# Attention of a two-layer graph network: two visits a round with eight heads each in place of four with four

## The chip, the cores and the metric

The kernel runs on one core of one Trainium2 chip. The metric is device time in microseconds (us) of one execution. Engines are named as the profile names them: PE is TensorE, with PEld its weight loads; DVE is VectorE, ACT is ScalarE, POOL is GpSimd, SP is SyncE, which here issues the transfers. SBUF and PSUM are the two on-chip memories; PSUM is used as eight banks of 128 x 512 numbers.

## The reference

64 graphs of 256 nodes with 512 features share one adjacency matrix. Cut to what matters:

```python
# x (64, 256, 512), adj (256, 256), all float32; 8 heads of 64
h = relu(layernorm(x))
q, k, v = h @ Wq + bq, h @ Wk + bk, h @ Wv + bv
scores = einsum('bqhd,bkhd->bhqk', q, k) / 8 + (1 - adj) * -1e9
x = x + einsum('bhqk,bkhd->bqhd', softmax(scores), v) @ Wo + bo
h = relu(layernorm(x))
hW = h @ W
e = leaky_relu(hW @ a1 [:, :, None] + hW @ a2 [:, None, :], 0.2) * adj
x = x + elu(softmax(e) @ hW + beta * hW)
```

## The kernel before

The graphs are worked off in 32 pairs. Every large product (Q and K, V, the output projection O, and W of the second layer) is done for a pair of graphs in Strassen's way (the Winograd form): seven block products, called `p(1)` to `p(7)` of a `Unit`, in place of eight. For a pair `p` the units are `UnitQK(p, 0)` and `UnitQK(p, 1)` (`ua`, `ub`), `UnitV(p)` (`uv`), `UnitO(p)` (`uo`) and `UnitW(p)` (`uw`). The block sums of the left operand are made by `combine_31`, `combine_2` and `combine_4` (L304, L308 and others).

A product is eight matmul records of PE of 256 columns (a float32 matmul of the code shows as two records). It goes to one PSUM bank. Products 2 and 3 have none of their own: they add into the banks of products 1 and 5. So product 3 can start only when the results that need product 5 alone have been read from that bank; for Q and K `put2` does this (L374, on DVE), and `put2` in turn needs the sum `u3` (L288).

Attention is done per graph `b` and half `q` of the heads (four heads). `scores(b, q)` makes four score tiles on PE (L420, two heads side by side in tiles of 64 x 128), then exp on ACT (L424), the product with the mask on POOL (L425) and the sum of the two halves on POOL (`pp`, L427). `values(b, q)` weighs V with them (`av`, L438, four heads side by side in tiles of 128 x 32), adds up the softmax sums (`sm`, L447), and leaves on DVE the reciprocal (L449), a running sum (L450) and the normalized output (`oT`, L452); a second running sum (L453) is put on POOL by the caller, through `between`, behind the second head of the scores that follow.

A *visit* is one `values` followed by the `scores` of the next graph or half. In the steady state a *round* handles one pair in `first_half(p)` and `second_half(p)`, with four visits in it. The order of PE, DVE, ACT and POOL is the order in which the code is written (`manual_schedule`): each engine takes its instructions in that order and waits where an input or a buffer isn't ready. In a round the stages of three pairs are mixed: Q, K and V of pair p+1, attention of pair p, O and the normalization of pair p-1, and the second layer's W of pair p-2.

Between the second visit of `second_half` and the next rounds, the second layer of pair p-1 is prepared: `y_stats` (L248) and `y_scales` (L255 on DVE, L258 to L260 on POOL) give mean and deviation, `y_normal` (L507, ACT) the normalized rows `h2`, `y_sums` (L513, DVE, tile `pr`) two weighted sums of each row, `gat_scores`, `gat_exp` and `divide` the attention weights of the second layer, `gat_t` their transposes (L546), `gat_z` the product with `h2` (`pz`, L559). Transfers stand on SP's queue in program order: `x` (in `load`), the same rows once more as `y` for the residual (`residual`, which also adds a bias on POOL, L470), and the results.

Tiles of one tag share a fixed number of buffers (`BUFS`, L58). A tile takes over a buffer of an older one and waits until that is no longer read. PSUM has eight banks under one tag.

Of the kernel before, what the change touches and what calls it, by code (L numbers as in the profile page):

```python
# [11 lines left out]
ALU = mybir.AluOpType  # L12
# [11 lines left out]
def kernel(ctx: ExitStack, tc: tile.TileContext, x, adj, wq, bq, wk, bk, wv, bv, wo, bo, w, a, beta, out):  # L24
# [33 lines left out]
    BUFS = {"set": 13, "qk": 8, "v": 4, "pt": 4, "xt": 4, "y": 8, "h2": 4, "e": 2, "eT": 2, "m": 2, "c": 3, "u": 4}  # L58

    def blk(tag, name):  # L60

        return sb([P, 2, N], tag, name, BUFS[tag])

# [12 lines left out]
    def load(p, *which):  # L76
        for g in [2 * p + gi for gi in which or (0, 1)]:
            for t in range(NT):
                XT[g, t] = sb([P, D], "xt", f"x_{g}_{t}", BUFS["xt"])
                nc.sync.dma_start(XT[g, t], x[g, t * P:(t + 1) * P, :])  # L80
# [213 lines left out]
    def combine_31(s, a21, a22, tag="set"):  # L294

        s["tag"] = tag
        s[7] = blk(tag, f"s3_{s['name']}")
        a21(s[7], ALU.subtract, s[1])
        s[5] = blk(tag, f"s1_{s['name']}")
        a22(s[5], ALU.add, s["a21"])  # L300
# [112 lines left out]
    def scores(b, q, between=None):  # L413
        pss = [bank(f"sc_{b}_{q}_{i}") for i in range(4)]
        for pair in range(2):
            qk = QK.pop((b, 2 * q + pair))
            for k in range(NT):
                for h in range(2):
                    hs = slice(h * HD, (h + 1) * HD)
                    nc.tensor.matmul(pss[2 * pair + h][:, k * N:(k + 1) * N], qk[hs, 1, k * P:(k + 1) * P],  # L420
                                     qk[hs, 0, :], start=True, stop=True)
        for i in range(4):
            pt = PT[b, q, i] = blk("pt", f"pt_{b}_{q}_{i}")
            nc.scalar.activation(pt, two(pss[i]), AF.Exp, scale=QSCALE)  # L424
            nc.gpsimd.tensor_tensor(pt, pt, maskT, ALU.mult)  # L425
            pp = PP[b, q, i] = sb([P, N], "pp", f"pp_{b}_{q}_{i}", 4)
            nc.gpsimd.tensor_tensor(pp, pt[:, 0, :], pt[:, 1, :], ALU.add)  # L427
            if between and i in between:
                between[i]()
# [12 lines left out]
    def values(b, q):  # L442

        ps = weigh(V.pop((b, q)), [PT.pop((b, q, i)) for i in range(4)], f"{b}_{q}")
        sums = bank(f"sm_{b}_{q}")
        for i in range(4):
            nc.tensor.matmul(sums[i * HH:(i + 1) * HH, :N], ones[:, :HH], PP.pop((b, q, i)), start=True, stop=True)  # L447
        rec = sb([P, N], "rec", f"rec_{b}_{q}")
        nc.vector.reciprocal(rec, sums[:, :N])  # L449
        nc.vector.tensor_tensor(acc, sums[:, :N], acc, ALU.add)  # L450
        OT[b, q] = blk("set", f"oT_{b}_{q}")
        nc.vector.tensor_tensor(OT[b, q], two(ps), rec.unsqueeze(1).to_broadcast([P, 2, N]), ALU.mult)  # L452
        return lambda: nc.gpsimd.tensor_tensor(acc, acc, rec, ALU.add)  # L453
# [48 lines left out]
    def normal(g, rstd, nmr, tag="h2"):  # L502
        h2 = H2[g] = [sb([P, D], tag, f"h2_{g}_{t}", BUFS[tag]) for t in range(NT)]
        SC[g] = sb([P, NT, 2], "s12", f"s12_{g}", 3)
        for t in range(NT):
            for f in range(2):
                nc.scalar.activation(h2[t][:, f * N:(f + 1) * N], Y[g, f][:, t, :], AF.Relu, bias=nmr[:, t:t + 1],  # L507
                                     scale=rstd[:, t:t + 1])
# [68 lines left out]
    class UnitW(Unit):  # L577

        def __init__(self, p, tags=("m", "c")):
            self.pair, self.o, self.tags = p, {}, tags  # L580
            super().__init__(f"w_{p}", nodes_mm(A.pop(("z", p)), WW))

        def elu(self, gi, fh, src, o=None, step=None):
            g = 2 * self.pair + gi
            if not step:
                m = blk(self.tags[0] if (gi, fh) != (0, 0) else "m", f"m_{g}_{fh}")
                nc.scalar.activation(m, src, AF.Relu, scale=-1.0)
                nc.scalar.activation(m, m, AF.Exp, scale=-1.0)  # L588
                self.o[gi, fh] = (o or blk(self.tags[1], f"o_{g}_{fh}"), m)
            if step is not False:  # L590
                nc.vector.scalar_tensor_tensor(self.o[gi, fh][0], src, 0.0, Y.pop((g, fh)), op0=ALU.max, op1=ALU.add)

        def finish(self, gi, fh, eng):
            g = 2 * self.pair + gi
            o, m = self.o[gi, fh]
# [10 lines left out]
        def put2_sums(self):  # L606
            self.c = blk(self.tags[1], f"o_{2 * self.pair + 1}_1")
# [77 lines left out]
    def residuals(p, tag="y"):  # L685
        for gi, fh in ((0, 0), (1, 1), (1, 0), (0, 1)):
            residual(p, gi, fh, tag)
# [26 lines left out]
    def start():  # L714
# [42 lines left out]
        scores(0, 0)  # L757
# [4 lines left out]
        shift(2)  # L762
        products(uv, 3)
        return wo_blocks

    def first():
        add = values(0, 0)
        scores(0, 1, {1: add})
        x_t(1)
        load(2)  # L770
        s = A["h", 1]
        ua, ub, uv = UnitQK(1, 0), UnitQK(1, 1), UnitV(1)
        ua.p(1)
        combine_24(s)
        products(ua, 4, 6)
        prods = project_a()
        prods(0)
        products(ua, 2, 7)
        add = values(0, 1)
        scores(1, 0, {1: add})  # L780
        residuals(0)
        products(ua, 5)
        ub.p(1)
        prods(1)
        products(ub, 4)
        products(ua, 3)
        products(ub, 6)
        prods(2)
        products(ub, 2)
        add = values(1, 0)  # L790
        scores(1, 1, {1: add})
        products(ub, 7, 5)
        uv.p(1)
        products(ub, 3)
        prods(3)
        prods(4)
        products(uv, 4)
        for i in range(2 * NT):
            x_stats(2, i)
        add = values(1, 1)  # L800
        x_scales(2)
        scores(2, 0, {1: add})
        o_blocks(0)
        products(uv, 6, 2)
        x_normals(2, *range(2 * NT))
        products(uv, 7, 5)
        prods(5)
        products(uv, 3)
        combine_24(A["o", 0])
        uo = UnitO(0)  # L810
        uo.p(1)
        uo.p(4)
        add = values(2, 0)
        scores(2, 1, {1: add})
        products(uo, 6, 2)
        return uo


    def first_half(p):
        g0, g1 = 2 * p, 2 * p + 1  # L820
        uw = UnitW(p - 2)
        uw.p(1)
        x_stats(p + 1, 0)
        x_stats(p + 1, 1)
        uw.p(4)
        x_stats(p + 1, 2)
        x_stats(p + 1, 3)
        products(uw, 6, 2, 7, 5)
# [3 lines left out]
        add = values(g0, 0)  # L832
        scores(g0, 1, {1: add})
# [3 lines left out]
        uo = UnitO(p - 1)  # L837
        uo.p(1)
# [8 lines left out]
        products(uo, 2)  # L847
        return uo

    def second_half(p, uo):  # L850
        g0, g1 = 2 * p, 2 * p + 1
        products(uo, 7)
# [3 lines left out]
        if p + 2 < NP:  # L856
            load(p + 2)
        products(uo, 3)
        combine_2(A["h", p + 1])
        add = values(g0, 1)  # L860
        y_stats_1(p - 1)
        y_stats_2(p - 1)
        combine_4(A["h", p + 1])
        scores(g1, 0, {1: lambda: (add(), y_scales(p - 1))})
        ua, ub = UnitQK(p + 1, 0), UnitQK(p + 1, 1)
        products(ua, 1, 4)
        y_normal(p - 1, 1)
        products(ua, 6)
        y_sums(p - 1, 1, 0, 1)
        products(ua, 2)  # L870
# [3 lines left out]
        add = values(g1, 0)  # L874
        scores(g1, 1, {1: add})
        products(ua, 3)
        y_sums(p - 1, 0, 1)
        products(ub, 1, 4, 6)
        gat_scores(g1 - 2)
        products(ub, 2)  # L880
        gat_exp(g1 - 2)
        gat_scores(g0 - 2)
        gat_exp(g0 - 2)
        products(ub, 7)
        divide(p - 1)
        products(ub, 5)
        add = values(g1, 1)
        scores(g1 + 1, 0, {1: add})
        if p == NP - 2:
            o_blocks(p, "xt")  # L890
        residuals(p)
        uv = UnitV(p + 1)
        uv.p(1)
        gat_t(g1 - 2)
        gat_t(g0 - 2)
        products(ub, 3)
        products(uv, 4, 6, 2, 7, 5)
        if p == NP - 2:
            return uv
        gat_z(p - 1)  # L900
        products(uv, 3)
        combine_24(A["z", p - 1])

    def last(uv):
        p = NP - 1
        g0, g1 = 2 * p, 2 * p + 1
        combine_24(A["o", p - 1])
        add = values(g0, 0)
        scores(g0, 1, {1: add})
        products(uv, 3)  # L910
# [3 lines left out]
        add = values(g0, 1)  # L914
        scores(g1, 0, {1: add})
        products(uo, 5)
        y_stats_1(p - 1)
        gat_z(p - 2)
# [3 lines left out]
        combine_24(A["z", p - 2])  # L922
        add = values(g1, 0)
        scores(g1, 1, {0: lambda: y_normal(p - 1, 1), 1: add})
        uw = UnitW(p - 2, ("pt", "xt"))
        products(uw, 1, 4)
        y_sums(p - 1, 1, 0, 1)
        products(uw, 6)
# [3 lines left out]
        residual(p, 0, 0, "qk")  # L932
        gat_scores(g1 - 2)
        gat_exp(g1 - 2)
        uw.p(5)
        uw.put2_sums()
        add = values(g1, 1)
        o_blocks(p)
        residual(p, 1, 1, "qk")
        residual(p, 1, 0, "qk")  # L940
        residual(p, 0, 1, "qk")
        add()
# [10 lines left out]
    def end(uw, uo):  # L953
        p = NP - 1
        g0, g1 = 2 * p, 2 * p + 1
        products(uo, 2)
        gat_scores(g0 - 2)
        gat_exp(g0 - 2)
        uo.p(6)
# [13 lines left out]
        normal(g1, rstd, minus(mr, f"y{g1}"), "qk")  # L973
# [6 lines left out]
        normal(g0, rstd, minus(mr, f"y{g0}"), "qk")  # L980
# [6 lines left out]
        uw = UnitW(p - 1, ("pt", "xt"))  # L987
# [16 lines left out]
        uw.put2_elu()  # L1004
        uw.p(3)
        gat_t(g0)
        uw.put12()
# [9 lines left out]
        uw = UnitW(p, ("pt", "xt"))  # L1017
# [16 lines left out]
    with tc.manual_schedule(engines={ENG.PE, ENG.DVE, ENG.Activation, ENG.Pool}):  # L1034
        WO = start()
        WW = {}
        uo = first()
        second_half(1, uo)
        for p in range(2, NP - 1):
            uv = second_half(p, first_half(p))  # L1040
        end(*last(uv))
# [16 lines left out]
    def general(src, dst, W, mask):  # L1058
        xt = sb([P, NT, D], "x", "fx", 1)
# [145 lines left out]
```

## Time and profile before

| what | value |
|---|---|
| median of three runs | 2856.71 us (2855.55 to 2857.03) |
| the profiled execution | 2857.51 us, its span 2855.7 us |
| mean granted TensorE clock | 0.997 |
| one round (from the av at 1009.24 to the one at 1097.33) | 88.09 us |
| busy in that round: PE, DVE, ACT, POOL | 88.09, 63.74, 32.63, 50.41 us |
| starts of the visits in and around it (av) | 1009.24, 1024.02, 1040.97, 1077.35, 1097.33 us |
| number of L449 (one for each `values`) | 128 |

How to read it: the span is the time from the first to the last instruction of the profiled execution, and the runs that are timed have no profile. A busy share says how much of the span an engine was at work, not whether others waited for it. A line of the timeline has the start in us, the length in us, engine, line of the code, operation, written tile and read tiles, sizes and how many instructions are merged; brackets give the idle time ahead of it and what ended it. The lengths of matmuls overlap, so their pace is read from the starts.

### The profile page before, as it was taken

To read this page: it belongs to the slowest core of one execution; us is meant where nothing else is said; L and a number is where in the kernel's file an instruction comes from. 1 tells how busy PE (TensorE), PEld (TensorE's weight loads), DVE (VectorE), ACT (ScalarE), POOL (GpSimd) and SP (SyncE) were. 2 spreads that over 40 slices of the span, in tenths; PEclk is the share of its full clock that TensorE was granted. 3 is DMA by queue.
4 is the path that set the end of the run, shared out by engine and by line. 5 is a ranking of instruction groups with operands and counts; after the bars stand their busy time and mean duration, and the time that the engine had idled before them with its cause. 6 is when DMAs were issued, how large, how long until landed. Compare 5 with 4: busy or idle time off the path is not lost. (4 is left out here: it accounts for less than half of the span.)

```text
span 2855.7 us, 46364 instructions
## 1 busy us (share of the span) xinstructions
PE 2837.8 (99%) x18110; PEld 2331.3 (82%) x18110; DVE 2067.1 (72%) x3651; ACT 1045.4 (37%) x2116; POOL 1624.5 (57%) x1592
## 2 busy tenths in 40 slices
PE   9999999999999999999999999999999999999997
PEld 8888888888888888888888888888888888888876
DVE  6776786767867677767777676786767877677767
ACT  3333433333433334333333333343333433334333
POOL 3755655556555556555575555655556655556572
PEclk9999999999999999999999999999999999999998
DMA  5000111100111001110011110111100111001001
GB/s 155 23 31 22 38 45 45 45 15 32 45 45 45 19 27 45 45 45 28 18 45 45 45 33 20 38 45 45 45 16 30 45 45 45 21 25 45 30 20 42
DMA packets 96479, 110.00 MB, mean 39 GB/s; under 512 B 8576, under 2 KB 79488, under 8 KB 96256
## 3 DMA queue, kind: packets, MB, share of 16 engines
q1 hardware_dynamic: 96256, 106.99, 12.0%
q8 instruction: 145, 2.38, 0.4%
q14 instruction: 78, 0.64, 0.1%
HBM read 73.41 MB, written 33.55 MB: 37 GB/s over the span
## 5 line engine op out<-in xcount | busy, mean ns | idle before, releaser
L425 POOL TENSOR_TENSOR pt<-pt,maskT 128x512 f32<-128x512 f32 x512 | 719.0, 1404 | 552.8 <-ACT pt L424 552.8
L427 POOL TENSOR_TENSOR pp<-pt 128x256 f32<-128x256 f32 x512 | 432.9, 845 | 40.2
L424 ACT ACTIVATE pt<-sc 128x512 f32<-128x512 f32 x512 | 264.4, 603 | 338.2 <-PE sc L420 332.0
L513 DVE SCALAR_TENSOR_TENSOR pr<-h,war 128x512 f32<-128x512 f32 x256 | 303.4, 1228 | 57.0 <-ACT h L507 57.0
L596 POOL TENSOR_TENSOR o<-o,m 128x512 f32<-128x512 f32 x40 | 50.6, 1268 | 515.1 <-ACT m L588 463.4
L420 PE MATMUL sc<-qk 64*128 64x256 f32 x2048 | 255.7, 389 | 0.0
L438 PE MATMUL av<-pt,v 128*32 128x256 f32 x4096 | 247.6, 382 | 0.0
L420 PEld LDWEIGHTS sc<-qk 64*128 64x128 f32 x2048 | 187.3, 186 | 69.7 <-PE av L438 38.3
L559 PE MATMUL pz<-eT,h 128*128 128x256 f32 x1024 | 226.8, 379 | 1.3 <-ACT eT L547 1.3
L449 DVE RECIPROCAL rec<-sm 128x256 f32<-128x256 f32 x128 | 223.3, 1745 | 3.5 <-PE sm L447 3.5
L559 PEld LDWEIGHTS pz<-eT,h 128*128 128x128 f32 x1024 | 194.9, 190 | 28.2 <-ACT eT L547 1.6
L438 PEld LDWEIGHTS av<-pt,v 128*32 128x32 f32 x4096 | 120.0, 109 | 108.4 <-issue 31.5
L356 PE MATMUL qk_p<-s_h,wq_t 128*128 128x256 f32 x768 | 197.4, 379 | 0.0
L356 PE MATMUL qk_p<-s_h,wk_t 128*128 128x256 f32 x768 | 197.1, 379 | 0.0
L389 PE MATMUL o_p<-wo_t,s_o 128*128 128x256 f32 x768 | 178.8, 383 | 0.2 <-ACT pt L424 0.2
L389 PE MATMUL w_p<-w_t,s_z 128*128 128x256 f32 x768 | 176.4, 379 | 0.3 <-DVE s_z L304 0.3
L389 PE MATMUL v_p<-wv_t,s_h 128*128 128x256 f32 x768 | 176.3, 379 | 0.0
L389 PEld LDWEIGHTS o_p<-wo_t,s_o 128*128 128x128 f32 x768 | 147.5, 192 | 21.3 <-ACT pt L424 0.9
L562 ACT COPY z<-pz 128x512 f32<-128x512 f32 x128 | 74.8, 586 | 244.2 <-PE pz L559 244.2
L573 DVE TENSOR_TENSOR s_z<-pz,z 128x512 f32<-128x512 f32 x64 | 44.1, 691 | 163.5 <-ACT z L562 163.5
L389 PEld LDWEIGHTS v_p<-wv_t,s_h 128*128 128x128 f32 x768 | 145.8, 190 | 20.1 <-ACT pt L424 0.3
L389 PEld LDWEIGHTS w_p<-w_t,s_z 128*128 128x128 f32 x768 | 145.6, 190 | 20.3 <-issue 0.6
(171 smaller groups left out, 5718.8 us busy)
## 6 DMA issues: line engine op xcount, KB each, us to landing
x<-in_x_dram SPq DMA_DIRECT2D x128, 256.0 KB, 3.6
y<-in_x_dram SPq DMA_DIRECT2D x128, 256.0 KB, 2.9
out_dram<-o SPq DMA_DIRECT2D x127, 256.0 KB, 2.2
wq_b<-in_L_gnn_Wq_dram SPq DMA_DIRECT2D x4, 256.0 KB, 5.4
wk_b<-in_L_gnn_Wk_dram SPq DMA_DIRECT2D x4, 256.0 KB, 5.6
wv_b<-in_L_gnn_Wv_dram SPq DMA_DIRECT2D x4, 256.0 KB, 4.9
wo_b<-in_L_gnn_Wo_dram SPq DMA_DIRECT2D x16, 64.0 KB, 3.3
w_b<-in_L_gnn_W_dram SPq DMA_DIRECT2D x4, 256.0 KB, 3.4
```

The lines of the kernel that those rows point to most:

```text
L356: nc.tensor.matmul(ps[:, j * N:(j + 1) * N], wj[i][:, c, ft * P:(ft + 1) * P], s[i][:, c, :], start=(start and j == 0 and c == 0), stop=(c ...
L389: nc.tensor.matmul(ps[:, t * N:(t + 1) * N], s[i][:, c, t * P:(t + 1) * P], wj[i][:, c, :], start=(start and t == 0 and c == 0), stop=(c = ...
L420: nc.tensor.matmul(pss[2 * pair + h][:, k * N:(k + 1) * N], qk[hs, 1, k * P:(k + 1) * P], qk[hs, 0, :], start=True, stop=True)
L424: nc.scalar.activation(pt, two(pss[i]), AF.Exp, scale=QSCALE)
L425: nc.gpsimd.tensor_tensor(pt, pt, maskT, ALU.mult)
L427: nc.gpsimd.tensor_tensor(pp, pt[:, 0, :], pt[:, 1, :], ALU.add)
L438: nc.tensor.matmul(ps[i * HH:(i + 1) * HH, s * N:(s + 1) * N], v[:, k, c0:c0 + HH], pts[i][:, k, :], start=(k == 0), stop=(k == NT - 1))
L449: nc.vector.reciprocal(rec, sums[:, :N])
L513: nc.vector.scalar_tensor_tensor(pr, H2[g][t], 1.0, war[:, j, :], op0=ALU.mult, op1=ALU.mult, accum_out=SC[g][:, t, j:j + 1])
L559: nc.tensor.matmul(ps[:, f * N:(f + 1) * N], h2[k][:, fs], eT[:, k, :], start=(k == 0), stop=(k == NT - 1))
L562: nc.scalar.copy(dst, two(ps))
L596: eng.tensor_tensor(o, o, m, ALU.add)
```

## The change

`scores(b, q)` and `values(b, q)` become `scores(b)` and `values(b)`, each of which does both halves, eight heads, one after the other. The round has two visits instead of four: `values(g0)` and `scores(g1)` in `second_half`, behind the output unit, and `values(g1)` and `scores(g1 + 1)` at its end, behind `ub`. The work that stood between the four visits is put between the two: V, the second layer's `gat_t` and `gat_z`, W and most of O now fill `first_half`; all of `ua` and `ub` follow the first visit, with product 1 of `ub` ahead of product 3 of `ua`.

The second running sum of `values` moves from POOL to DVE. `y_scales` stands behind the third head of the first half. Buffers change: `pt` and `pp` have 8 instead of 4, `y` 6 instead of 8; `h2` loses its own four buffers and shares the four of the inputs `x`, so the loads of the next inputs are issued behind `gat_z`, in `first_half`; `combine_31` adds in place; in the last pairs the second layer's output is written over `y` or into other tags. The loops at the start (`start`, `first`) and the end (`last`, `end`) are rearranged in the same way.

```diff
-    BUFS = {"set": 13, "qk": 8, "v": 4, "pt": 4, "xt": 4, "y": 8, "h2": 4, "e": 2, "eT": 2, "m": 2, "c": 3, "u": 4}
+    BUFS = {"set": 13, "qk": 8, "v": 4, "pt": 8, "x": 4, "y": 6, "e": 2, "eT": 2, "m": 2, "c": 3, "u": 4}
...
-    def scores(b, q, between=None):
+    def scores(b, between={}):
+        for q in range(2):
...
-            pp = PP[b, q, i] = sb([P, N], "pp", f"pp_{b}_{q}_{i}", 4)
+                pp = PP[b, q, i] = sb([P, N], "pp", f"pp_{b}_{q}_{i}", 8)
...
-    def values(b, q):
+    def values(b):
+        for q in range(2):
...
-        return lambda: nc.gpsimd.tensor_tensor(acc, acc, rec, ALU.add)
+            nc.vector.tensor_tensor(acc, acc, rec, ALU.add)
...
-    def normal(g, rstd, nmr, tag="h2"):
+    def normal(g, rstd, nmr, tag="x"):
...
     def first_half(p):
-        g0, g1 = 2 * p, 2 * p + 1
+        uv = UnitV(p)
+        products(uv, 1, 4)
+        gat_t(2 * p - 3)
+        gat_t(2 * p - 4)
+        products(uv, 6, 2, 7, 5)
+        gat_z(p - 2)
+        load(p + 1)
+        residuals(p - 1, ((0, 0), (1, 1)))
+        products(uv, 3)
+        combine_24(A["z", p - 2])
         uw = UnitW(p - 2)
-        uw.p(1)
+        products(uw, 1, 4, 6)
         x_stats(p + 1, 0)
...
         o_blocks(p - 1)
         x_scales(p + 1)
-        add = values(g0, 0)
-        scores(g0, 1, {1: add})
+        residuals(p - 1, ((1, 0), (0, 1)))
...
     def second_half(p, uo):
...
         products(uo, 3)
-        combine_2(A["h", p + 1])
-        add = values(g0, 1)
+        values(g0)
+        combine_24(A["h", p + 1])
         y_stats_1(p - 1)
         y_stats_2(p - 1)
-        combine_4(A["h", p + 1])
-        scores(g1, 0, {1: lambda: (add(), y_scales(p - 1))})
+        scores(g1, {(0, 2): lambda: y_scales(p - 1)})
         ua, ub = UnitQK(p + 1, 0), UnitQK(p + 1, 1)
-        products(ua, 1, 4)
+        products(ua, 1, 4, 6)
         y_normal(p - 1, 1)
-        products(ua, 6)
+        products(ua, 2)
         y_sums(p - 1, 1, 0, 1)
-        products(ua, 2)
         y_normal(p - 1, 0)
         products(ua, 7, 5)
         y_sums(p - 1, 0, 0)
-        add = values(g1, 0)
-        scores(g1, 1, {1: add})
+        ub.p(1)
         products(ua, 3)
         y_sums(p - 1, 0, 1)
-        products(ub, 1, 4, 6)
+        products(ub, 4, 6)
         gat_scores(g1 - 2)
-        products(ub, 2)
         gat_exp(g1 - 2)
+        ub.p(7)
         gat_scores(g0 - 2)
         gat_exp(g0 - 2)
-        products(ub, 7)
+        products(ub, 5)
         divide(p - 1)
-        products(ub, 5)
-        add = values(g1, 1)
-        scores(g1 + 1, 0, {1: add})
...
-        products(ub, 3)
-        products(uv, 4, 6, 2, 7, 5)
...
+        products(ub, 2, 3)
+        values(g1)
+        scores(g1 + 1)
```

## The prediction

> **What bounds the kernel now.** First the page, for the engine that has no room:
>
> ```profile
> span 2855.7 us, 46364 instructions
> PE 2837.8 (99%) x18110; PEld 2331.3 (82%) x18110; DVE 2067.1 (72%) x3651; ACT 1045.4 (37%) x2116; POOL 1624.5 (57%) x1592
> L513 DVE SCALAR_TENSOR_TENSOR pr<-h,war 128x512 f32<-128x512 f32 x256 | 303.4, 1228 | 57.0 <-ACT h L507 57.0
> ```
>
> TensorE (PE) is never out of work, so only two things count: how many array turns its queue takes, and whether some other engine makes it wait. Second, the timeline of PE through one visit, the one in `second_half` (`values(g0, 1)`, then `scores(g1, 0)`), in a middle round:
>
> ```profile
> 1007.42 1.89 PE L389 MATMUL o_p<-wo_b,s_o 128*128 128x256 f32 x8
> 1009.24 1.93 PE L438 MATMUL av<-pt,v 128*32 128x256 f32 x32
> 1010.99 0.61 PE L447 MATMUL sm<-pp,ones 128*32 128x256 f32 x8
> 1011.54 2.00 PE L420 MATMUL sc<-qk 64*128 64x256 f32 x16
> 1013.47 1.13 PE L356 MATMUL qk_p<-h,wq_b 128*128 128x256 f32 x4
> 1014.43 1.03 PE L356 MATMUL qk_p<-h,wk_b 128*128 128x256 f32 x4
> 1015.29 1.03 PE L356 MATMUL qk_p<-h,wq_t 128*128 128x256 f32 x4
> ...
> ```
>
> Columns are start and length. Starts tell the pace: a plain group of four takes 1015.29-1014.43 = 0.86, so one turn is 0.216 and a product of eight is 1.73. (A matmul of the code shows as two records; av and sm run four records a turn, sc two.) Third, VectorE (DVE) and GpSimd (POOL) in the same stretch:
>
> ```profile
> 1011.75 1.76 DVE L449 RECIPROCAL rec<-sm 128x256 f32<-128x256 f32 x1
> 1013.43 0.36 DVE L450 TENSOR_TENSOR acc<-sm,acc 128x256 f32<-128x256 f32 x1
> 1013.70 0.68 DVE L452 TENSOR_TENSOR oT<-av,rec 128x512 f32<-128x512 f32 x1
> 1014.30 2.05 DVE L248 BATCH_NORM_STATS2 st_y<-y 128x6 f32<-128x256 f32 x6
> ...
> 1022.72 1.74 DVE L513 SCALAR_TENSOR_TENSOR pr<-h,war 128x512 f32<-128x512 f32 x1
> ...
> 1026.95 0.48 DVE L374 SCALAR_TENSOR_TENSOR qk<-qk_p,bq,qk_u 128x256 f32<-128x256 f32 x1
> ```
> ```profile
> 1013.43 1.27 POOL L425 TENSOR_TENSOR pt<-pt,maskT 128x512 f32<-128x512 f32 x1 [7.98 <-ACT pt L424]
> 1014.79 0.72 POOL L427 TENSOR_TENSOR pp<-pt 128x256 f32<-128x256 f32 x1
> 1015.47 1.26 POOL L425 TENSOR_TENSOR pt<-pt,maskT 128x512 f32<-128x512 f32 x1
> ...
> 1020.01 0.20 POOL L260 TENSOR_TENSOR mr_y<-mv_y,rstd_y 128x4 f32<-128x4 f32 x1
> ...
> 1022.20 1.72 POOL L425 TENSOR_TENSOR pt<-pt,maskT 128x512 f32<-128x512 f32 x1
> ```
>
> Look at 1022.20: the mask product takes 1.72 instead of 1.27, and the `pr` that starts at 1022.72 takes 1.74, where one beside an idle POOL takes 0.68 (1026.15 less 1025.54 is 0.61 start to start). An operation of DVE that reads two SBUF tensors and an operation of POOL wait for each other, in turns. From the starts: a `pr` behind a mask product costs 1.67, behind a `pp` sum 1.15, alone 0.61.
>
> **What is removed: changes of tile shape.** In the rows above, product to av takes 1.82 (1.73 and 0.09), av to sm 1.75 (0.02), sm to sc 0.55 for two turns of 0.43 (0.12), sc to product 1.93 (0.20), the product's first half 0.96 (0.10). A visit pays 0.53 beyond its turns. 128 visits become 64; the second half of each new visit follows in the same shape and pays none of it. 64 x 0.53 = 34 us off PE's own path. The count of matmuls is the same. The range of this term is 30 to 36.
>
> **What the doubled scores do to PSUM.** With t = 0 at the first av, the new visit has av, sm, av, sm to t = 4.46, eight score banks to 8.11, then products. In the changed kernel's built order the fifth and sixth score tiles take the banks of sm and av of q = 0, the seventh and eighth those of the first two scores. sm and av are free after reciprocal 1.68, sum 0.27 and oT 0.68, from t = 2.45: 5.1; they are wanted at 6.3. The first exps end at 6.3 and 6.8 (exp begins 1.22 after sc starts, four take 2.07); they are wanted at 7.15. Cost nothing; if exp were 0.4 later it would be that much a visit.
>
> **What moves on POOL and SP.** `acc` plus `rec` (L453) goes from POOL to DVE: 109 us off POOL, which does not set the end. Eight heads are 16 to 20 us of POOL after a visit (2.04 uncontended, 2.46 with DVE); the next `values` is 24 to 46 us away, so PE does not wait for `pt`. The four `x` loads now wait for the pz matmuls (buffers shared with h2). They land 3.6 after issue, at about t = 30 after the second visit of a round; their first reader, `x_stats`, stands behind the second layer's third product, t = 33. On SP nothing urgent stands behind them: the next y loads wait for an output step at t = 36. Cost nothing, with 3 us of cover.
>
> **What is added: a burst on DVE in front of a product.** This decides. In `second_half` the product `ua` 3 adds into the bank that `put2` (L374) must first read, in both kernels. Before, a visit of 4.2 us stood between `ua` 5 and `ua` 3; now only `ub` 1 (1.73) does. PE reaches `ua` 3 at 8.11 + 0.10 + 7 x 1.73 = 20.3. DVE's order from the visit on is: reciprocal, L450, L452, the moved L453, all twice; L304 and L308; six L248, four L255; L285; four `pr`; L288; L374. Step by step:
>
> - First reciprocal at 2.45 (DVE must end `put12`; before 2.51). One set is 1.68 + 0.27 + 0.60 = 2.55; L453 on DVE I bound by 0.28 (L450's spacing) and 1.4 (behind a mask product). The first meets POOL idle: 0.33, the second reciprocal is at 5.33 and its L453 at 7.88.
> - POOL begins its mask product at 6.34 (1.89 after sc). So the second L453 waits for `pp` (0.72), L304 for a mask product (1.67), L308 for `pp` (1.15): 11.42. Stats 1.96, aggregates 0.41: 13.8.
> - POOL computes rstd behind the third head and these: 13.9; mr is 1.37 later (1018.64 to 1020.01), the first `pr` 1.60 after mr (1020.01 to 1021.61): 16.9.
> - Four `pr` against POOL's remaining five heads: 1.07 + 1.67 + 1.15 + 1.67 = 5.56: 22.4. Before, they took 4.54, the last alone.
> - L288 to L374 0.80, two L374 0.87: 24.1.
>
> PE waits 24.1 - 20.3 = 3.8; say 3.9 with the release. The next such point, `ub` 3, is reached by the same queue at t = 34.5 while PE, already late, comes at 35.0: nothing more. Bounds: with every turn lost to a mask product 2.3 more, 6.2; with no turn lost at all L374 ends at 19.6, wait 0. I take 3.9, since the turns are what the rows show.
>
> **What the wait does to the clock.** Before has one gap of this size, near its end:
>
> ```profile
> 2790.47 0.47 PE L171 MATMUL pe<-ident,s 128*128 128x128 f32 x1 [3.99 <-DVE pr L513]
> 2790.74 7.76 PE L389 MATMUL o_p<-wo_t,s_o 128*128 128x256 f32 x24
> ```
>
> The 24 records behind it take 7.76 where 24 turns take 5.34: 2.4 lost; the stretch 2789.0 to 2795.4 had a granted clock of 0.50. Ends for this term are 0 and 2.4 a wait; I take 1.2, since not each gap will fall as that one did.
>
> The Trainium skill (TensorE: Matmul & The Clock Gate, Part 1) says the clock halves after at least one idle window of about 3.4 us, free-running. By it only one gap in five or so holds a whole window, an estimated 0.4 a wait, or some 2956 us at the end; the row above, where the clock fell though PE had worked in part of the window, speaks for more.
>
> **Sum.** The burst occurs in `second_half` for p = 1 to 30, and `first` has one like it (sums and products of W in place of `pr`): 31 times. Span 2855.7 - 34 + 31 x (3.9 + 1.2) = 2979.8. The profiled run took 2857.51 outside for its 2855.7; the median, 2856.71, is 1.0 above the span: 2981.
>
> **Rivals.**
> 1. Faster: DVE keeps ahead. Place: `ua` 3; price: none, the 34 us stay. It needs L374 before t = 20.3, thus `pr` near 0.6 each and L304/L308 unhindered. For it: POOL idle for part of a round (57% busy). Against: the turns at 1022. Time 2855.7 - 34 + 1 = 2823. Up to 1.1 of wait a round stays below the old time. 14%.
> 2. The wait is there, the clock holds: 2855.7 - 34 + 31 x 3.9 + 1 = 2944. For it: a gap may straddle windows. 28%.
> 3. Gain and wait cancel (about 1.1 a round): 2851 to 2862. 4%, of it 3% within 0.2%.
> 4. DVE loses each turn and the clock falls each time: 31 x (6.2 + 2.4) = 267, so 3089. 9%.
>
> My forecast has 45%, own range 2955 to 3035. To hold 8 in 10 the range takes in rival 2 and shorter waits (1.4 a round, 2866) and ends at 3035, where 6.9 a round stands.
>
> Under 0.2% (5.7 us) is no change. Slower 83%, same 3%, faster 14%.
>
> **What would show it.** In the changed profile: PE's idle before L356, released by DVE L374, of 3 to 5 us about 30 times; `pr` at a mean above 1.3 us; granted clock below 0.99; visits of av, sm, av, sm, sc with 0.53 of change each. A round (two visits) of about 92, where before has 88.09. I am wrong if PE shows no such wait, or if scores wait for banks or POOL's `pt` instead.

## The result, and the profile after

| | before (run beside it) | changed kernel |
|---|---|---|
| median | 2856.13 us | 3033.76 us (3033.29 to 3034.11) |
| span of the profiled execution | 2855.7 us | 3032.3 us |
| mean granted clock | 0.997 | 0.973 |
| a steady round | 88.09 us | 93.27 us (mean of 29) |
| from the first busy instruction to the third group of `tr` (pair 2) | 124.53 us | 136.86 us |
| from the last group of `tr` to the end of the last matmul | 168.06 us | 182.54 us |

The ratio is 1.0623 (95% interval 1.0604 to 1.0641): slower by 6.2%. The spans differ by 176.6 us: 29 rounds x 5.18 = 150.3, the start 12.3, the end 14.5, less 0.5 for what follows the last matmul (7.8 us in place of 8.3).

First the page of the changed kernel: span, busy time, and two groups of its list (busy and mean ns of one; then idle time ahead of them and what ended it).

```profile
span 3032.3 us, 46347 instructions
...
PE 2885.5 (95%) x18110; PEld 2392.4 (79%) x18110; DVE 2083.6 (69%) x3779; ACT 1037.7 (34%) x2116; POOL 1517.9 (50%) x1464
...
L515 DVE SCALAR_TENSOR_TENSOR pr<-h,war 128x512 f32<-128x512 f32 x256 | 298.0, 1208 | 77.4 <-ACT h L509 77.4
...
L356 PE MATMUL qk_p<-s_h,wq_b 128*128 128x256 f32 x256 | 94.7, 507 | 118.3 <-DVE qk L374 118.3
```

The matmul count is the same, PE's share has fallen from 99% to 95%, and one group of matmuls now stands behind 118.3 us of idle time. Before, that group had no such wait (the list by shapes):

```profile
L356 PE MATMUL qk_p<-s_h,wq_b 128*128 128x256 f32 x256 | 68.9, 392 | 0.0
```

The waits of PE in the changed kernel, from the view that adds them up by who is waited for (us in total, times, longest):

```profile
PE qk_p L356 <- DVE qk L374: 118.3, 31, 5.5
PE o_p L389 <- ACT o_u L283: 7.2, 2, 3.7
PE at L548 <- DVE e L539: 3.6, 1, 3.6
PE o_p L389 <- DVE oT L454: 2.4, 1, 2.4
```

31 waits at one place, one at each `ua` 3 of the pairs 1 to 31 (pair 0, in `start`, has none), and a few more that occur once or twice: those belong to the start and the end. Now one of the 31, in the timelines of PE, DVE and POOL (start, length; in brackets the idle time ahead and what ended it). The first av of this visit is at 1073.78.

```profile
1093.21 1.03 PE L356 MATMUL qk_p<-h,wk_b 128*128 128x256 f32 x4
1098.01 2.07 PE L356 MATMUL qk_p<-s_h,wq_b 128*128 128x256 f32 x4 [3.76 <-DVE qk L374]
```
```profile
1090.68 1.18 DVE L515 SCALAR_TENSOR_TENSOR pr<-h,war 128x512 f32<-128x512 f32 x1 [2.51 <-ACT h L509]
...
1091.79 1.75 DVE L515 SCALAR_TENSOR_TENSOR pr<-h,war 128x512 f32<-128x512 f32 x1
...
1093.47 1.21 DVE L515 SCALAR_TENSOR_TENSOR pr<-h,war 128x512 f32<-128x512 f32 x1
...
1094.61 1.74 DVE L515 SCALAR_TENSOR_TENSOR pr<-h,war 128x512 f32<-128x512 f32 x1
...
1096.28 0.68 DVE L288 TENSOR_TENSOR qk_u<-qk_p,qk_u 128x512 f32<-128x512 f32 x1
1097.07 0.49 DVE L374 SCALAR_TENSOR_TENSOR qk<-qk_p,bq,qk_u 128x256 f32<-128x256 f32 x1
1097.47 0.48 DVE L374 SCALAR_TENSOR_TENSOR qk<-qk_p,bk,qk_u 128x256 f32<-128x256 f32 x1
```
```profile
1090.59 0.73 POOL L429 TENSOR_TENSOR pp<-pt 128x256 f32<-128x256 f32 x1
1091.27 1.72 POOL L427 TENSOR_TENSOR pt<-pt,maskT 128x512 f32<-128x512 f32 x1
1093.07 1.06 POOL L429 TENSOR_TENSOR pp<-pt 128x256 f32<-128x256 f32 x1
1094.09 1.71 POOL L427 TENSOR_TENSOR pt<-pt,maskT 128x512 f32<-128x512 f32 x1
```

Each `pr` begins 0.1 to 0.5 us behind an operation of POOL and comes out longer than the 0.68 it takes alone: 1.2 beside a `pp`, 1.75 beside a mask product. POOL's operations are stretched too, all but the first of these: 1.06 for a `pp` of 0.73, 1.72 for a mask product of 1.27. PE has finished `ub` 1 at 1094.1 and starts `ua` 3 when the second L374 ends, at 1098.0. (The text counts a wait from the end of the last turn, 0.216 behind its start; the bracket counts from the modelled end of the last matmul, so the 3.93 us of the text stand there as 3.76.) And PE restarts slowly: its first group of four takes 1.86 from start to start of the next in place of 0.96. The view by stretches shows why (length, PE busy and count, then PEld, DVE, ACT and POOL busy, the granted clock, DMA share and GB/s):

```profile
1090.66:1094.08 3.42, 3.42 (x17) 2.82 (x15) 3.40 (x5) 3.42 (x8) 3.34 (x3) 1.00 0.00 0
1094.08:1097.49 3.41, 0.16 (x1) 0.00 (x0) 3.29 (x7) 0.79 (x2) 3.33 (x4) 1.00 0.00 0
1097.49:1100.90 3.41, 2.90 (x7) 2.33 (x8) 3.41 (x7) 0.00 (x0) 3.25 (x4) 0.50 0.00 0
1100.90:1104.32 3.42, 3.42 (x18) 3.01 (x17) 2.38 (x8) 0.00 (x0) 0.87 (x1) 1.00 0.00 0
```

The clock is at one half (0.50) for one stretch of 3.41 us, here the one in which the wait ends; in every third round it is two such stretches. There is one in each of the 29 steady rounds, 129.7 us in sum; before there is none in them.

A round of the changed kernel is 5.18 us longer by these parts, from the starts of PE's records: fewer shape changes -1.07; a wait of 0.17 for DVE at `uo` 3 and 0.10 at its restart, +0.27; the wait at `ua` 3, 3.93, and 0.10 at its restart; the clock, 1.95 (1.93 as e4 measures it below).

### The profile page after: what moved, and what is told of

Same layout as the page of the kernel before. It is cut to its first block, busy times and chain, and to the rows that moved or that the text cites. A ratio compares the mean times of both kernels' runs of the same rounds, so it can differ in the third digit from the quotient of the medians.

```text
span 3032.3 us, 46347 instructions
## 1 busy us (share of the span) xinstructions
PE 2885.5 (95%) x18110; PEld 2392.4 (79%) x18110; DVE 2083.6 (69%) x3779; ACT 1037.7 (34%) x2116; POOL 1517.9 (50%) x1464
## 4 chain that ended last, share of the span: by engine, by line
## 5 line engine op out<-in xcount | busy, mean ns | idle before, releaser
L429 POOL TENSOR_TENSOR pp<-pt 128x256 f32<-128x256 f32 x512 | 413.4, 807 | 40.1
L515 DVE SCALAR_TENSOR_TENSOR pr<-h,war 128x512 f32<-128x512 f32 x256 | 298.0, 1208 | 77.4 <-ACT h L509 77.4
L356 PE MATMUL qk_p<-s_h,wq_b 128*128 128x256 f32 x256 | 94.7, 507 | 118.3 <-DVE qk L374 118.3
L532 ACT ACTIVATE e<-e 128x256 f32<-128x256 f32 x128 | 52.2, 408 | 449.4 <-DVE e L527 449.4
L356 PEld LDWEIGHTS qk_p<-s_h,wq_b 128*128 128x128 f32 x256 | 58.6, 242 | 139.3 <-DVE qk L374 130.7
L472 POOL TENSOR_TENSOR y<-y,bo 128x512 f32<-128x512 f32 x128 | 161.6, 1286 | 0.0
L285 DVE TENSOR_TENSOR v_u<-v_p,v_u 128x512 f32<-128x512 f32 x32 | 22.1, 692 | 181.4 <-PE v_p L389 181.4
L356 PE MATMUL qk_p<-h,wq_t 128*128 128x256 f32 x512 | 143.7, 407 | 0.0
L356 PE MATMUL qk_p<-h,wq_b 128*128 128x256 f32 x512 | 134.7, 386 | 0.3 <-ACT h L333 0.3
L356 PE MATMUL qk_p<-h,wk_t 128*128 128x256 f32 x512 | 133.9, 384 | 0.0
L509 ACT ACTIVATE h<-y,nmr_y,rstd_y 128x256 f32<-128x256 f32 x256 | 132.5, 591 | 1.1
```

The costliest lines, as they stand in the source:

```text
L356: nc.tensor.matmul(ps[:, j * N:(j + 1) * N], wj[i][:, c, ft * P:(ft + 1) * P], s[i][:, c, :], start=(start and j == 0 and c == 0), stop=(c ...
L472: nc.gpsimd.tensor_tensor(r, r, bo2[:, fh * N:(fh + 1) * N].unsqueeze(1).to_broadcast([P, 2, N]), ALU.add)
L515: nc.vector.scalar_tensor_tensor(pr, H2[g][t], 1.0, war[:, j, :], op0=ALU.mult, op1=ALU.mult, accum_out=SC[g][:, t, j:j + 1])
```

## The experiments

Each is compared with the kernel before on the same chip; e9 is timed in five rounds, the others once. The first four start from the changed kernel and take one suspect each.

**e1: the running sum back on POOL.**

```diff
-            nc.vector.tensor_tensor(acc, acc, rec, ALU.add)
+            LATER.append(lambda rec=rec: nc.gpsimd.tensor_tensor(acc, acc, rec, ALU.add))
...
+        while LATER:
+            LATER.pop(0)()
```

> The changed kernel with the second running sum (acc plus rec) back on GpSimd, behind the eight heads of the scores that follow, so that VectorE's row in front of the product ua 3 has two operations less. Theory (the row of VectorE work, stretched by turns with GpSimd, holds ua 3): the sums cost VectorE 0.33 and 0.72 us, but GpSimd is behind its third head only at t = 13.4 us anyway, so 0.4 to 1.0 us of the 3.8 us wait goes, 30 times: 3000 to 3022 us. Rival A (the moved sum is the cause of the loss): the wait goes, 2870 us or less. Rival B (the wait is for PSUM banks or for masked scores): no change, 3030 to 3036 us.

Measured: 3004.75 us, a round 92.20 us, the wait at `ua` 3 3.32 us, one stretch of half clock in each round. The sum moved to DVE is thus 0.6 us of the 3.9: real, and not the cause. (In the start the change did harm: the wait at `ua` 3 grew to 11.4 us there, and the third `tr` came 7.7 us later.)

**e2: two products of `ub` ahead of `ua` 3.**

```diff
-        ub.p(1)
+        products(ub, 1, 4, 6)
         products(ua, 3)
         y_sums(p - 1, 0, 1)
-        products(ub, 4, 6)
```

> The changed kernel with the products ub 4 and ub 6 ahead of ua 3, so that 3.5 us more of TensorE work stand between the point where ua 3's bank is asked for and ua 3. Theory (VectorE's work between the two visits is longer than TensorE's, wherever TensorE meets it): the wait at ua 3 falls from 3.8 to under 1 us, but waits of 1 to 2.5 us each appear at the transposes pe of the first graph and at ub 3, about 3.4 us a round in all; being short they leave the clock at full speed more often: 2930 to 2975 us. Rival A (only the place of ua 3 is at fault): no wait comes back, 2840 to 2870 us. Rival B (the release of the bank is bound to TensorE's own order): same wait, 3030 us.

Measured: 2956.98 us, a round 90.81 us. Its waits of PE:

```profile
PE pe L171 <- DVE pr L515: 54.3, 30, 1.8
PE qk_p L356 <- DVE qk L374: 33.9, 61, 5.5
```

3.5 us more of work in front of `ua` 3 took 3.45 us from its wait, but 2.7 us of it came back: 1.87 us at the transposes `pe`, behind the last `pr`, and 0.80 us at `ub` 3. DVE's burst is late as a whole, so later points of the same queue catch it. In the rounds the clock never fell: none of their waits is longer than 1.9 us. Most of the 77 us gained is the clock (29 x 1.93 = 56 by e4 below).

**e3: POOL free during the burst.** For odd graphs the mask product and the half sum are left out (the first half of `pt` stands for `pp`), so the softmax of these graphs isn't the reference's.

```diff
+                if b % 2:
+                    PP[b, q, i] = pt[:, 0, :]
+                    if (q, i) in between:
+                        between[q, i]()
+                    continue
                 nc.gpsimd.tensor_tensor(pt, pt, maskT, ALU.mult)
```

> The changed kernel without GpSimd's mask product and half sum for the odd graphs (the scores of a round's first visit); the sums of these graphs are taken over the first half of the keys, and the attention of the odd graphs is not masked. VectorE's work is the same. Theory (turns with GpSimd stretch VectorE's row): unhindered, the aggregates end at t = 11.8, pr begins at 14.9 and takes 0.61 each, put2 has read the bank at 19.0, before TensorE comes at 20.3: no wait at ua 3, round of 87.0 to 87.6 us, 2835 to 2860 us in all. Rival (VectorE has too much work in front of ua 3 even when alone, or the clock or banks are the cause): a wait of 1.4 us or more stays, 2880 us or more.

Measured: 2843.61 us, a round 87.30 us. The group of `pr` on its page:

```profile
L520 DVE SCALAR_TENSOR_TENSOR pr<-h,war 128x512 f32<-128x512 f32 x256 | 166.7, 698 | 28.6 <-ACT h L514 28.6
```

698 ns against 1208, and no wait at `ua` 3. Not one instruction of DVE was taken away; only POOL's stream beside it. So the wait is the two engines slowing each other, and 87.30 is what a round takes without it: 0.79 below before, the 1.07 of the shape changes less the 0.27 at `uo` 3. That `y_scales` stands behind POOL's third head is not part of it: in the changed kernel POOL was done with that head and waited 0.5 us for DVE (L258 for L255) in every round.

**e4: the wait filled with matmuls.** Eight matmuls of the code into a bank that nothing reads, between `ub` 1 and `ua` 3.

```diff
         ub.p(1)
+        ps, h = bank(f"fill_{p}"), A["h", p + 1]
+        for n in range(8):
+            nc.tensor.matmul(ps[:, :N], WQ[1][:, n % 2, :P], h[1][:, n % 2, :], start=True, stop=True)
         products(ua, 3)
```

> The changed kernel with sixteen turns of matmuls (3.45 us) into a free PSUM bank between ub 1 and ua 3; nothing reads them. They fill most of the time in which TensorE waits and change nothing else in the order. Theory (part of the loss is the clock that halves behind the wait): the wait at ua 3 shrinks to 0.3 us or so, ua 3 starts at the same distance from the visit, the granted clock stays at 1.0 in the rounds, and 2.3 us a round come back: 2955 to 2975 us. Rival (the clock costs little and the wait is all): 3025 to 3040 us.

Measured: 2970.81 us, a round 91.34 us, a wait of 0.48 us left and no half clock in the rounds. PE does 3.5 us more work for nothing and the kernel is 63 us faster than the changed one, 56 of them in the rounds: 93.27 - 91.34 = 1.93 us a round is the price of the clock alone.

**e6: the kernel before with its cover taken away.** `ua` 3 ahead of the third visit; nothing else differs from before.

```diff
+        products(ua, 3)
         add = values(g1, 0)
         scores(g1, 1, {1: add})
-        products(ua, 3)
```

> The kernel before, with one thing moved: ua 3 goes ahead of the third four-head visit, in the steady rounds. Four heads with four stay, and all of VectorE's work keeps its order but for the two copies of ua 3. Theory (the third visit, 4.2 us of PE, was what covered the copies that ua 3 waits for): in the kernel before VectorE's second L374 ends at 1115.9 and ua 3 starts at 1116.3 with the visit from 1112.1 in front of it, so without that the wait is 3.8 us, half clock comes with each as it did in the changed kernel, a round takes 93.0 to 94.2 us, and the time is 3000 to 3040 us. Rival 1 (it is the eight heads with eight, which make VectorE later, that cost the time): the wait is under 1.5 us and the time below 2910 us. Rival 2 (the wait comes but the clock holds): 2960 to 2990 us.

Measured: 3009.8 us, 154 us above before. The wait at `ua` 3 is 3.95 us (3.8 was expected), in each of the 29 rounds. So a single move costs 154 us, without any eight-head visit: in the kernel before DVE was late already, and the visit between `ua` 5 and `ua` 3 covered it. Before, in the round that the prediction shows:

```profile
1023.07 1.03 PE L356 MATMUL qk_p<-s_h,wk_t 128*128 128x256 f32 x4
1027.35 0.47 DVE L374 SCALAR_TENSOR_TENSOR qk<-qk_p,bk,qk_u 128x256 f32<-128x256 f32 x1
1028.24 1.13 PE L356 MATMUL qk_p<-s_h,wq_b 128*128 128x256 f32 x4
```

PE is done with `ua` 5 at 1023.93, the second L374 ends 3.9 us later, and the visit lasts 4.3. In the changed kernel the second L374 ends 5.6 us behind `ua` 5, and `ub` 1 covers 1.73 of them. So of its 3.93 us, 2.2 come from the lost cover alone and 1.7 from DVE being later than before: rival 1 falls as the main cause, but it has a share.

But the clock did not do as expected: it fell 13 times, for 75.1 us in all, and in 16 of the 29 rounds (of 92.14 us) it held through the same wait. Two of these waits in the view by stretches, cut at the edges at which this run's clock changes (PE busy and count, granted clock, DMA):

```profile
1343.74:1347.16 3.42, 1.41 (x7) 1.00 0.00 0
1347.16:1350.57 3.41, 1.63 (x8) 1.00 0.00 0
1435.91:1439.32 3.41, 1.38 (x7) 1.00 0.00 0
1439.32:1442.73 3.41, 1.63 (x4) 0.50 0.00 0
1442.73:1446.15 3.42, 3.42 (x22) 0.50 0.00 0
```

The waits are alike; what differs is 0.02 us in how the first stretch is shared between work and idleness (by the starts 2.17 us of it idle in the one, 2.19 in the other). The last section comes back to this.

**e10: a shorter fill.** To test that reading: e4 with five matmuls, which leave 1.75 us idle.

```diff
-        for n in range(8):
+        for n in range(5):
```

> e4 with five matmuls as fill in place of eight: ten records, 2.2 us, in front of ua 3. They write a bank that nothing reads. Of the wait of 3.9 us some 1.8 us is left idle. Theory (half clock comes after a window of 3.413 us in which PE was idle for 2.18 us or more, as the waits of e6 and of the changed kernel showed by their place in the windows): the clock holds in the steady rounds, a round takes 91.3 us as e4's, and the time is 2967 to 2976 us. Rival (any wait of more than some 1 to 1.5 us that cuts a window costs half clock, as the 1.8 us wait near the end of the kernel before seemed to): half clock in a good part of the rounds, 2985 us or more.

Measured: 2970.85 us, a round 91.30 us, no half clock in the rounds. Three matmuls less of fill made 1.3 us more of wait a round and no difference of time. The rival falls.

**e5: DVE's burst spread.** The other experiments say what to do: keep the `pr` away from in front of L374.

```diff
     # second_half
         products(ua, 2)
-        y_sums(p - 1, 1, 0, 1)
         y_normal(p - 1, 0)
         products(ua, 7, 5)
-        y_sums(p - 1, 0, 0)
+        y_sums(p - 1, 1, 0)
         ub.p(1)
         products(ua, 3)
-        y_sums(p - 1, 0, 1)
+        y_sums(p - 1, 1, 1)
...
         products(ub, 5)
-        divide(p - 1)
+        y_sums(p - 1, 0, 0)
+        divide(g1 - 2)
     # first_half
-        products(uv, 1, 4)
...
+        uv.p(1)
+        y_sums(p, 0, 1)
+        uv.p(4)
+        gat_t(g1)
+        uv.p(6)
+        gat_scores(g0)
+        gat_exp(g0)
+        products(uv, 2, 7)
+        divide(g0)
+        products(uv, 5)
+        gat_t(g0)
+        z_graph(p, 1)
...
+        z_graph(p, 0)
```

> The changed kernel with the four products of the second graph taken from in front of the second layer's put (half of them go behind ub 1, half of them behind ua 3), and one first-graph row half, its gat scores, its exponential and its division moved into the first half of the next round, where VectorE has idle time. Nothing is left out. Theory (the wait at ua 3 is VectorE's burst, not PE or a buffer): VectorE's copy that ua 3 waits for ends about 20.2 us after the first weighted value against 20.3 for PE, so the wait at ua 3 falls below 0.6 us, the clock stays at 1.0 in the steady rounds, a round takes 87.3 to 88.0 us (the 88.09 of before less the 0.95 of fewer shape changes, plus up to 0.8 of small waits), and with the 12 and 14.5 us that start and end lost the whole takes 2845 to 2875 us. Rival (VectorE's work is conserved and the wait only moves, to ub 3, to the transposes or to z): a wait of 2 us or more appears elsewhere in a round, and the time is 2900 us or above.

Measured: 2881.49 us, a round 88.25 us. DVE in one round, its first av at 1111.66:

```profile
1128.71 0.69 DVE L288 TENSOR_TENSOR qk_u<-qk_p,qk_u 128x512 f32<-128x512 f32 x1 [2.66 <-PE qk_p L356]
1130.44 0.48 DVE L374 SCALAR_TENSOR_TENSOR qk<-qk_p,bq,qk_u 128x256 f32<-128x256 f32 x1 [1.04 <-PE qk_p L356]
1130.84 0.47 DVE L374 SCALAR_TENSOR_TENSOR qk<-qk_p,bk,qk_u 128x256 f32<-128x256 f32 x1
```

The second L374 ends 19.65 us after the first av, before PE comes (20.3): the wait is gone, and L374 now waits for PE. The same instructions of DVE are in the round, so the rival (work conserved, wait only moved) falls; but the round missed its 88.0 by 0.25 and the time its 2875 by 6, since 0.9 us of wait a round had come up at the transposes of the second layer's weights, behind the division (L539).

**e7 and e8: that wait, the start and the end.** e7 puts the transposes behind the first z blocks, and in `first` the sums and products of W behind `ua` 3 and the o blocks and x scales between POOL's heads; e8 also puts the last `values` ahead of products w 2 and 7.

```diff
     # e7, first
-        products(ua, 1, 4, 6)
-        prods = project_a()
-        prods(0)
-        products(ua, 2, 7, 5)
+        products(ua, 1, 4, 6, 2, 7, 5)
         ub.p(1)
-        prods(1)
         products(ua, 3)
+        prods = project_a()
...
-        scores(2)
-        o_blocks(0)
+        scores(2, {(0, 2): lambda: o_blocks(0), (0, 3): x_scale})
     # e8, last
+        values(g1)
         products(uw, 2, 7)
...
         uw.put2_sums()
-        values(g1)
```

> The spread kernel of before (e5), with two more orders changed and nothing left out. In the first half of a round the transposes of the second graph's weights go behind the first four z blocks, and V's last product behind them, so that neither waits for the division. In the start, the weight sums and the four groups of weight products go behind VectorE's copies for ua 3, and POOL makes the o blocks and the scales of x behind the third and fourth head of the eight and not behind the eighth. Theory: the 0.80 us a round that PE waits at the transposes goes, a round takes 87.4 to 87.6 us; in the start the waits of 5.5, 1.5 and 3.5 us and two stretches of half clock go, so the third tr comes at 124 to 126 us in place of 137.0; with e5's end the whole takes 2840 to 2856 us. Rival (the start is as long for another reason, one that the order does not move, such as the loads of the weights): the third tr stays above 132 us and the time above 2850 us.

> e7 with the end changed too: the last weighted values go ahead of the products w 2 and 7, so that these and w 5 and w 3 lie between them and the output unit, and the first output product's copy on ACT goes ahead of the elu's activations. Nothing is left out. Theory: the waits of 2.5 us for oT and 3.9 us for o_u in the end go, and with them a stretch of half clock worth 1.7 us; some of it comes back at the transposes that wait 3.7 us for the division, so the time is 3 to 9 us below e7, 2833 to 2852 us. Rival (the chain of VectorE to the last division sets the end and the waits only move): within 2 us of e7.

Measured: e7 2842.45 us, a round 87.29 us, the third `tr` at 126.4 us. The round is now the 87.30 of e3, with POOL's work in it. The start is 0.4 us above the bound given: `ub` 3 now waited 4.0 us, released by L374, which stood behind the products of W on DVE. e8: 2842.76 us; its rival was right. The waits for `oT` and `o_u` went, and 5.4 us of wait for `put2_sums` came: DVE has no room there.

**e9: the best version.** The rounds of e7, the products of W spread, and in the end the first output copy ahead of ACT's exponentials and the division ahead of DVE's second combination.

```diff
     # last and end, against e7
-        gat_exp(g1 - 2)
-        uw.put2_elu(False)
         uw.p(3)
         uo = UnitO(p)
         uo.p(1)
+        gat_exp(g1 - 2)
+        uw.put2_elu(False)
...
-        uo.p(6)
         gat_scores(g0 - 2)
         gat_exp(g0 - 2)
+        uo.p(6)
         uw.put2_elu(True)
+        divide(g1 - 2, g0 - 2)
```

> The spread kernel with e7's rounds and e8's idea for the end in another form. Start: the weight sums stay behind ua 3, and the four groups of weight products are spread over the time in which VectorE has no copy that PE waits for, with their transposes last. End: the first output product and its copy go ahead of the exponential and the elu's activations, the second graph's gat scores go ahead of output product 6, and the last division ahead of VectorE's second combination. Nothing is left out. Theory: the rounds stay at 87.30 us; in the start the wait of 4.0 us and its stretch of half clock go (third tr at 121 to 123 us in place of 126.4); in the end 2 us for o_u and 2 to 4 us for the division go, with a stretch of half clock; the time is 2829 to 2839 us, a ratio to before of 0.990 to 0.994. Rival (the start and the end are bound by VectorE's work, so the waits only move, as e8's did): 2840 to 2844 us.

Measured in five rounds: 2836.38 us (2835.78 to 2836.91), ratio to before 0.9932 (95% interval 0.9918 to 0.9945). Its page:

```profile
span 2834.5 us, 46444 instructions
...
PE 2811.1 (99%) x18110; PEld 2346.5 (83%) x18110; DVE 2098.4 (74%) x3779; ACT 1033.8 (36%) x2116; POOL 1535.8 (54%) x1464
...
L515 DVE SCALAR_TENSOR_TENSOR pr<-h,war 128x512 f32<-128x512 f32 x256 | 265.0, 1071 | 2.2 <-ACT h L509 2.2
```

PE is at 99% again with DVE busier than ever (74%), and the span is 21.2 us below before: 29 x 0.804 = 23.3 from the rounds and 0.7 from the start, less 2.9 in the end (from the last group of `tr` to the last matmul, 170.95) and 0.1 in rounding and in what follows it. The third `tr`, at 123.87, missed the 121 to 123 expected: two new waits of 1.2 and 1.8 us came up in the start. The idea of the change, fewer changes of shape, is worth what it costs only where the cover that it takes away isn't needed.

## Why the prediction came out as it did

The direction and the place were right. 2981 was forecast, with 2866 to 3035 around it; 3033.76 is 53 us above the one and inside the other by 1.2. That it lies inside is in part luck: the upper end was drawn for waits and clock of 6.9 us a round (5.18 and the 1.07 saved make 6.25) and not for a longer start and end. Step by step:

- **The burst on DVE: right, in nearly each step.** From the first av at 1073.78, in brackets the forecast: second reciprocal 5.53 (5.33), second L455 8.07 (7.88), stats 11.40 (11.42), rstd on POOL 13.92 (13.9), first `pr` 16.90 (16.9), L288 22.50 (22.4), second L374 done 24.17 (24.1). The 0.2 us by which the first steps came late went again because the second L455 cost 0.51 and not 0.72: two small errors that cancelled. The wait was 3.93 (3.9), at `ua` 3, released by L374, 30 times, and 5.7 in `first`. e3 and e5 show the mechanism: POOL away from the burst, or the `pr` away, and the wait is 0. e6 shows that the cover was the third visit, and that 1.7 us of the wait come from the longer burst. The bound "every turn lost", 6.2, was not needed.
- **Shape changes: right.** 64 x 0.53 = 34 was forecast, 1.06 a round; the starts show 0.535 a visit in both kernels, so 1.07 a round. What the forecast did not have is the wait and restart of 0.27 at `uo` 3.
- **PSUM, POOL and SP at nothing: right in the rounds.** No wait of PE on a bank, on `pt`, or of `x_stats` on the loads appears among the 29 rounds. L455 on DVE (e1) is 0.6 us of the wait.
- **The clock: the first step that failed.** "I take 1.2, since not each gap will fall as that one did": each did, and e4 measures 1.93 a wait, within the ends of 0 and 2.4. That is 0.73 x 29 = 21 us of the 53. The reason given is not wrong in itself, as e6 shows (16 of 29 held), but by the last section only one place on the clock's grid in eight holds a wait of this length, and the changed kernel never came to it. The rule weighed there, that a whole idle window of about 3.4 us is needed (the Trainium skill, TensorE: Matmul & The Clock Gate, Part 1), gave 0.4; these runs show half clock after stretches idle for 2.2 of 3.41 us. (A whole window would fit into a gap of 3.9 us at one place in seven, not in five.)
- **The sum: the second step that failed.** "31 times", with `first` "one like it", counted one burst for the start and none for the end. Start and end lost 26.3 us together, where the sum had 7.0 (two more waits of 5.1, less three rounds' shape changes): 19 us of the 53. The changed kernel's PE waits in the start:

```profile
82.48 2.08 PE L356 MATMUL qk_p<-s_h,wq_b 128*128 128x256 f32 x4 [5.50 <-DVE qk L374]
123.35 1.97 PE L389 MATMUL o_p<-wo_t,s_o 128*128 128x256 f32 x8 [1.51 <-DVE s_o L304]
128.81 3.78 PE L389 MATMUL o_p<-wo_b,oT 128*128 128x256 f32 x8 [3.50 <-ACT o_u L283]
```

  The first is the burst that was forecast, 5.7 us from the last turn and not 3.9. The others are POOL's eight heads in one piece: the o blocks and the scales of x stand behind them, ACT's x normals behind the scales, and the copy that PE needs behind the normals. "Cost nothing" was worked out for the rounds, where PE asks for POOL's next result 24 to 46 us after a visit; in the start it asks for the o blocks 17 us after the scores (105.2 to 121.8), when POOL is on the second of their two sums, begun only when its eighth head was done (119.9). e7, which puts both jobs between the heads, has neither wait (0.3 us at `uo` 6, none at `uo` 2).
- The rest, some 12 us: the 0.27 a round at `uo` 3, and at `ua` 3 0.03 of wait and 0.10 of restart (29 x 0.40).
- **The sign that did not come:** `pr` above 1.3 us in the mean. The four in front of L374 took 5.60 (5.56 forecast), but the mean over all was 1.208, below the 1.228 of before. Of a round's eight the last two run when POOL has no head left, at 0.68. A mean over a group hides the four that matter.

## What to carry to other kernels

Work between two instructions that depend on each other is cover, and its worth is not in its own row: before moving it, list who must be done by the time it ends, and walk that engine's queue step by step from the last common point; here that walk was right to 0.2 us at each step. A queue can be late as a whole and do no harm; more cover moved most of the wait (e2: 2.7 of 3.45 us came back), taking work from in front of the late instruction removed it (e5, with 0.9 us left elsewhere, which e7 removed). Count the start and the end as stages of their own, with their own cover, and price a wait of some microseconds on PE with its half clock.

## What the runs showed of the hardware

**What decides whether the clock falls.** In all these runs half clock begins and ends on a grid of 3.413 us that is fixed within a run. In the steady rounds of e6, with 29 waits of 3.95 us that lie differently on the grid (PE's idle time taken from the end of the last turn), the clock held wherever the idle time was at most 2.17 us in each stretch (2.17 and 1.78; 2.12 and 1.82; 2.04 and 1.92) and fell where one had 2.18 or more (2.18 and 1.76; 2.66 and 1.29; a whole 3.41). The waits of 3.92 in the changed kernel had 2.66 or more in one stretch each time, those of 3.3 in e1 2.47 or more; the waits of 1.87 in e2 and 1.75 in e10 can't reach it, and there the clock held in every round. So in the rounds PE had to be idle for about 64% of one stretch, not for all of it. A wait of 3.92 us holds the clock by this only if its first part is 1.75 to 2.17 us, one place on the grid in eight; of this range the runs show 2.04 to 2.17 alone.

**How long it stays low.** Behind a single wait the clock came back after one stretch where at most 0.58 us of the wait lay in the next one, and after two where it was 0.61 or more. This gives the price: in the changed kernel the rounds go through three places, with idle times of 2.83 and 1.09, 0.85 and 3.08, 3.41 and 0.51; half the work time of the low stretches is (6.83 - 1.09) / 2 = 2.9, 3.41 / 2 = 1.7 and (3.41 - 0.51) / 2 = 1.45, mean 2.0, where e4 measured 1.93. Each loss also shifts the next wait on the grid: in the changed kernel three rounds (93.01, 92.74 and 94.14 us) make 279.89 us, which is 82 stretches, so the same three places come back and none of them is one that holds. The rounds of 92.145 us in e6 are 26.996 stretches long, so its waits crept over the grid by some 0.01 to 0.02 us a round, and the clock held for twelve rounds on end, until 2.17 had become 2.19.

Not settled: outside of the rounds the clock fell with less idle time. In the start of e7 a wait of 4.0 us, split as 2.03 and 1.97, cost a stretch; in the end of e5 one of 1.93 and 1.80 did, with transposes in the rest of the second stretch; near the end of the kernel before one of 0.70 and 1.11, again beside transposes. So idle time on the grid is not the whole rule, and no run here tells what else counts.
